# A GRU and a mixture of experts on one core: block 0's projections summed in the gates' banks, two seeds picked by matmul, and the rows of the last eight tiles fetched early

## The chip, the core and the metric

The kernel runs on one core of a Trainium2 chip. The metric is the device time of one execution in microseconds (us), as the median of the runs. A core has five engines that run their own instruction queues in order: TensorE (PE in the profile, PEld for its weight loads), VectorE (DVE), ScalarE (ACT), GpSimd (POOL) and SyncE (SP). SP does no arithmetic here: it issues DMA transfers. ACT and POOL can issue them too. An instruction waits in its queue until the semaphores it needs are set, and everything behind it in that queue waits with it.

## The reference

A gated recurrent cell (GRU) runs over T = 256 time steps for B = 8 sequences of width D = 512; its outputs go through a mixture of 8 experts, two chosen for each token, and through a shared expert; the input is added back.

```python
def cell(h, x):
    gi = x @ W_ih + b_ih
    gh = h @ W_hh + b_hh
    i_r, i_z, i_n = jnp.split(gi, 3, axis=-1)
    h_r, h_z, h_n = jnp.split(gh, 3, axis=-1)
    r = jax.nn.sigmoid(i_r + h_r)
    z = jax.nn.sigmoid(i_z + h_z)
    n = jnp.tanh(i_n + r * h_n)
    return (1.0 - z) * n + z * h

# per token of the GRU's outputs:
topk_w, topk_ids = jax.lax.top_k(softmax(x @ w_gate), 2)      # weights scaled to sum to 1
routed = sum over the two experts of weight * (silu(x @ up_gate) * (x @ up)) @ down
shared = (silu(x @ sh_gate) * (x @ sh_up)) @ sh_down
out = input + routed + shared
```

## The kernel before

All arithmetic is in 32-bit floats. The order of every engine's instructions is the order of the program's text (a manual schedule).

**The GRU.** Time is cut into 16 blocks of `TS` = 16 steps. `project(k, g)` makes the input projection of block k for gate g (0, 1, 2 for r, z, n): four pieces, one for each quarter q of the input width, each of four matmuls of 512 columns into one PSUM bank. The end of the last piece adds the bias and puts the result into an SBUF tile (`gi_first` for block 0, `gi_later` for all others), from which it is sent to memory, turned to another layout. From there `load_seeds(c)` brings it back in chunks of `SC` = 4 steps into `seeds` (r and z) and `seeds_n` (n); each has two buffers. `open_gate(n, g)` has ACT copy one step's seed into the gate's part of a PSUM bank (`banks`: "rn", "z" and "x"), and `step(n)` adds the recurrent matmuls on top of it (L518), then works out the new state on ACT and DVE. `step(n)` calls `open_gate(n + 1, ...)` for the step after it. POOL makes one small copy in each step (`last_hn`, L547).

Other work is laid between the steps: each step is given a share of a queue of pieces (projections of coming blocks, the shared expert), and `afterward` puts small pieces of VectorE work behind a step where there is room.

**The head** is all that comes before step 0. SP loads x's block 0 (`load_x_plain(0)`), three quarters of the input weights, the biases, the last quarter, x's block 1, the recurrent weights, and block 2. TensorE runs all twelve pieces of block 0 in three banks of the pool `ps_mm`, and DVE adds the bias to each gate (L434). ACT sends chunk 0 to memory (`send_first`, L461 and L463); `load_seeds(0)` brings it back, the z part by ACT and the n part by POOL. Meanwhile TensorE turns block 1 (`turn_x_plain(1)`) and runs ten pieces of block 1's projections. Then the three gates are opened, ACT issues six more sends (chunks 1 to 3), and step 0 begins.

**The expert tiles.** During the recurrence the tokens are ranked and their rows dealt, by indirect DMAs, into a table in memory (`dealt`) that is sorted by expert. After the recurrence, up to 39 tiles of 128 rows are run; the first 35 (`always`) always run. `fetch_rows(i)` loads a register on SP with the place of tile i's rows and issues four DMAs of 64 KB, into one of the three buffers of the pool `xpool`. `tile_unit(i)` has five parts: `before_` (DVE turns the rows, L912, and SP fetches tile i + 2), four up-matmuls (L782; L791 for tile 34) into a bank, the gating on ACT and DVE (L769, L773, L774), a turn (L808, L810), and two down-matmuls (L947; L940 for tile 34), after which DVE scales the result into a tile `y` with two buffers (L950; L941 for tile 34) and POOL adds it into `out` by an indirect DMA (L956). `run_tile` interleaves three tiles: tile i's `before_`, tile i - 1's up-matmuls, tile i - 2's turn and down-matmuls.

The list `routing` holds what is done between the last pieces of the shared expert, `fetch_rows(0)` and `fetch_rows(1)` last. When four pieces are left, `before_` of tiles 0 and 1 is done. The shared expert's last two results go to `out` by SP's stores in `add_up` (L884), at the end of these pieces.

Of the kernel before, what the change touches and what calls it, by code (L numbers as in the profile page):

```python
# [9 lines left out]
F32 = mybir.dt.float32  # L10
# [3 lines left out]
ALU = mybir.AluOpType  # L14
# [4 lines left out]
TS = 16  # L19
SC = 4  # L20
NS = 2
NH = 4


@with_exitstack
def kernel(
# [108 lines left out]
    load_x_plain(0)  # L135
    for q in range(NQ):
        if q == NQ - 1:
            nc.sync.dma_start(bias, b_ih.partition_broadcast(P))
            nc.sync.dma_start(bias_h, b_hh[0 : 2 * D].partition_broadcast(P))
        nc.sync.dma_start(wih[:, q], w_ih.rearrange("(p q) n -> q p n", q=NQ)[q])  # L140
    load_x_plain(1)
    w_hh_v = w_hh.rearrange("(q p) n -> p q n", p=P)
    for g in (0, 2, 1):
        cols = slice(g * D, (g + 1) * D)
# [150 lines left out]
    for j in range(4):  # L295
# [4 lines left out]
    for tile_ in seeds_n:  # L300
        nc.gpsimd.tensor_copy(tile_, seed_hn.unsqueeze(1).broadcast_to([P, SC, P]))


    rows = dram.tile([B, T, D], F32, name="rows")
# [8 lines left out]
    nc.gpsimd.memset(nothing, 0.0)  # L313
    load((listed[0:P], vacant), (listed[P : E * NM + 1], vacant[0 : E * NM + 1 - P]))
    load((dealt[E * NM], nothing))


    spare = deque()
# [75 lines left out]
    def bank_of(shape, name):  # L394
        if len(held) == 3:
            for needed in held[0]:
                needed()
        readers = []
        held.append(readers)
        return ps_mm.tile(shape, F32, tag="mm", name=name), readers  # L400

    def catch_up(room):
        while afterwards and (room is None or afterwards[0][0] <= room):
            cost, work = afterwards.popleft()
            work()
            if room is not None:
                room -= cost

    def project(k, g):

        box = {}

        def issue(q, cols):
            if q == 0 and cols.start == 0:
                if k in turned_x:
                    turned_x.pop(k)()
                box["ps"], _ = bank_of([P, D], f"gip_{k}_{g}")
            multiply(
                box["ps"][:, cols],
                lambda c: xT_of[k][:, c, q, :],  # L420
                wih[:, q, g * D + cols.start : g * D + cols.stop],
                start=(q == 0 and cols.start == 0),
                stop=(q == NQ - 1 and cols.stop == D),
            )

        def by_group(t_):
            return t_.rearrange("p (q j i) -> p j q i", q=NQ, j=4)

        def end():
            gi = gi_later if k else gi_first  # L430
            to_gi = gi[:, :, g, :].rearrange("p j (q i) -> p j q i", q=NQ)
            bias_g = by_group(bias[:, g * D : (g + 1) * D])
            if k == 0:
                nc.vector.tensor_tensor(to_gi, by_group(box["ps"]), bias_g, ALU.add)  # L434
            else:
                nc.scalar.copy(to_gi, by_group(box["ps"]))
                nc.gpsimd.tensor_tensor(to_gi, to_gi, bias_g, ALU.add)
            if g > 0:
                projected.add((k, "rzn"[g]))
            if g > 0 and k == 0:  # L440
                send_first(g, 0)
            elif g > 0:
                to = gi_dram[k][g % 2].rearrange("j b t n -> (b t) j n")
                if g == 1:
                    nc.sync.dma_start(to.rearrange("p j (a n) -> p j a n", a=2), gi[:, :, 0:2, :])
                else:
                    nc.sync.dma_start(to, gi[:, :, 2, :])
# [6 lines left out]
    projected = set()  # L454

    def send_first(g, c):

        rows_ = slice(SC * B * c, SC * B * (c + 1))
        to = gi_first_dram[g % 2][c].rearrange("j t b n -> (t b) j n")
        if g == 1:  # L460
            nc.scalar.dma_start(to.rearrange("p j (a n) -> p j a n", a=2), gi_first[rows_, :, 0:2, :])  # L461
        else:
            nc.scalar.dma_start(to, gi_first[rows_, :, 2, :])  # L463

    def load_seeds(c, of="nz"):

        k, o = divmod(c * SC, TS)
        steps = slice(o, o + SC)
        for g in of:
            assert (k, g) in projected  # L470
            tile_, at_row = (seeds_n[c % NS], B) if g == "n" else (seeds[c % NS], 0)
            for j in range(4):
                if k:
                    src = gi_dram[k][int(g != "n")][j, :, steps, :]
                else:
                    src = gi_first_dram[int(g != "n")][o // SC, j].rearrange("t b n -> b t n")
                by = nc.sync if c else nc.scalar if g == "z" else nc.gpsimd
                row = 32 * j + at_row
                by.dma_start(tile_[row : row + B], src)

    def open_gate(n, g):

# [406 lines left out]
        )  # L889

    xr_of = {}

    def fetch_rows(i):
        if i < NT:
            xr_of[i] = xpool.tile([P, NG, P], F32, tag="x", name=f"xr_{i}")
            at = nc.values_load(
                laid["steer"][0:1, NT + 1 + i : NT + 2 + i],
                engines=(mybir.EngineType.SP,),
                min_val=0,
                max_val=E * NM,  # L900
            )
            src = dealt[bass.ds(at, 1)].rearrange("o (g t) (j m) -> j t (o g) m", g=NG, j=4)
            for j in range(4):
                nc.sync.dma_start(xr_of[i][32 * j : 32 * j + 32], src[j])

    def tile_unit(i):
        box = {}
# [98 lines left out]


    nc.vector.transpose(states[0].rearrange("p q b -> p (q b)"), h.rearrange("p q i -> p (q i)"))
    nc.vector.tensor_tensor(bias[:, 0 : 2 * D], bias[:, 0 : 2 * D], bias_h, ALU.add)

    first = [project(0, g) for g in range(3)]
    for q in range(NQ):
        for g in range(3):
            first[g][q].run(None)
    catch_up(None)
    load_seeds(0, "z")
    load_seeds(0, "n")
    load_shared()

    projections = deque()  # L1020
    for k in range(1, NB):
# [11 lines left out]
    ahead_of_it = 2 * NQ + 2  # L1033
    while ahead_of_it:
        piece = projections.popleft()
        ahead_of_it -= piece.parts > 0
        piece.run(None)
    for g in gate_of:
        open_gate(0, g)
    for c in range(1, TS // SC):  # L1040
        for g in (1, 2):
            send_first(g, c)
    load_seeds(1)
    due = spent = 0.0
    to_enter = deque()
    for k in range(NB):
# [4 lines left out]
        def when(t, cost, busy, work):  # L1051
            at.setdefault(t, []).append((cost, busy, work))
# [13 lines left out]
            for i in range(2):  # L1066
                when(12 + late + 2 * i, 0, 0, lambda k=k, i=i: deal_rows(k - 1, i))
        for e in range(E):
            when(2 + e, 0, 0, lambda k=k, e=e: nc.sync.dma_start(
                dealt[e * NM + k].rearrange("p (a n) -> p a n", n=P),  # L1070
                blank.unsqueeze(1).broadcast_to([P, D // P, P]),
            ))
# [130 lines left out]
```

## Time and profile before

| | us |
|---|---|
| Median of three runs | 1394.12 (1392.59 to 1395.21) |
| The profiled execution's own time | 1392.42 |
| Its span, first to last instruction | 1390.3 |
| TensorE busy | 1369.6 |
| VectorE, ScalarE, GpSimd busy | 654.6, 473.8, 290.1 |

| Stretch of the span (us) | What runs there |
|---|---|
| 0 to 31.84 | the head |
| 31.84 to about 1145 | the 256 steps |
| to 1190.3 | the rest of the shared expert, routing of the last block |
| 1190.3 to 1380.1 | the 35 expert tiles on TensorE |
| 1383.24 | the last scatter into `out` is issued |

A row of the timeline has the start, the duration, the engine, the line, the operation, what it writes and reads, how often (merged rows), and in brackets how long the engine stood idle before it and what ended that. An engine's name with a q (SPq, ACTq) marks what its queue issues rather than what its arithmetic does. A row of the waits has the engine and line that waited, what it waited for, the total in us, how often, and the longest. A row of the windows has the stretch, its length, the busy time of PE, PEld, DVE, ACT and POOL, the granted TensorE clock, the share of the DMA engines, and GB/s.

### The profile page before, as it was taken

How to read it: one execution, taken by the hardware profiler on the slowest of the kernel's cores; microseconds unless marked ns; L12 is line 12 of the kernel's file. 1: busy time of each engine (PE TensorE's matmuls, PEld its weight loads, DVE VectorE, ACT ScalarE, POOL GpSimd, SP SyncE). 2: the span in 40 equal slices, each digit the busy share in tenths (PEclk: the TensorE clock that was granted, in tenths of full speed). 3: DMA queues.
4: the chain of work that ended last, by engine and by line, in shares of the span. 5: the costliest groups of instructions: out<-in, count | busy, mean ns of one | idle time of the engine just before them, and what ended most of it. 6: DMA issues, size and time to landing. Idle time of an engine off the chain costs nothing. (4 is left out here: it accounts for less than half of the span.)

```text
span 1390.3 us, 59000 instructions
## 1 busy us (share of the span) xinstructions
PE 1369.6 (99%) x24524; PEld 784.1 (56%) x24524; DVE 654.6 (47%) x2702; ACT 473.8 (34%) x2037; POOL 290.1 (21%) x564
## 2 busy tenths in 40 slices
PE   8999999999999999999999999999999999999996
PEld 3455556665656565656665566566656665444443
DVE  2445444545454544455544554554445543344442
ACT  0444443434343434343434343434343330111110
POOL 3333332121111111111111111111111132133332
PEclk9999999999999999999999999999999999999999
DMA  7545563333332232223222223232223445455553
GB/s 272 161 139 144 124 134 98 112 104 91 101 101 67 74 83 75 67 83 83 81 77 59 83 77 88 58 84 83 66 67 83 131 101 168 93 94 102 96 99 52
DMA packets 157490, 137.36 MB, mean 99 GB/s; under 512 B 17240, under 2 KB 133384, under 8 KB 157224
## 3 DMA queue, kind: packets, MB, share of 16 engines
q1 hardware_dynamic: 140680, 95.54, 24.6%
q0 software_dynamic: 15072, 37.11, 12.1%
q8 instruction: 194, 3.18, 1.0%
q10 hardware_dynamic: 1472, 0.93, 0.3%
q14 instruction: 72, 0.59, 0.1%
HBM read 61.00 MB, written 72.52 MB: 96 GB/s over the span
## 5 line engine op out<-in xcount | busy, mean ns | idle before, releaser
L518 PE MATMUL ps_rn<-we,hT 128*8 128x256 f32 x8192 | 490.5, 379 | 5.6 <-DVE hT L549 3.0
L518 PEld LDWEIGHTS ps_rn<-we,hT 128*8 128x8 f32 x8192 | 223.2, 89 | 254.6 <-ACT ps_z L490 51.2
L531 DVE STREAM_TRANSPOSE rT<-ps_rn 128x128 f32<-128x128 f32 x256 | 81.2, 317 | 434.5 <-PE ps_rn L518 434.5
L518 PE MATMUL ps_z<-we,hT 128*8 128x128 f32 x8192 | 272.2, 273 | 0.0
L518 PEld LDWEIGHTS ps_z<-we,hT 128*8 128x8 f32 x8192 | 227.5, 90 | 50.7
L535 ACT ACTIVATE rT<-rT 128x32 f32<-128x32 f32 x256 | 58.5, 229 | 527.7 <-DVE rT L531 519.7
L547 POOL COPY last_hn<-hn 128x1 f32<-128x1 f32 x256 | 46.8, 183 | 826.2 <-DVE hn L546 826.2
L845 PE MATMUL gu_s<-hc,wsu 128*32 128x256 f32 x3072 | 188.4, 379 | 0.0
L342 PE MATMUL gip<-we,xT 128*32 128x512 f32 (+2 forms) x1872 | 186.1, 522 | 1.6 <-DVE xT L220 1.6
L845 PEld LDWEIGHTS gu_s<-hc,wsu 128*32 128x32 f32 x3072 | 101.2, 110 | 58.5 <-issue 11.8
L342 PE MATMUL po<-wsd,act_s 128*32 128x512 f32 (+2 forms) x1272 | 130.2, 509 | 0.0
L782 PE MATMUL gu_t<-we,xrT 128*128 x272 | 127.8, 593 | 0.0
L342 PEld LDWEIGHTS gip<-we,xT 128*32 128x32 f32 x1872 | 59.9, 111 | 71.3 <-issue 61.5
L531 DVE STREAM_TRANSPOSE zT<-ps_z 128x128 f32<-128x128 f32 x256 | 79.0, 309 | 0.0
L552 ACT COPY hc<-hT 128x32 f32<-128x32 f32 x192 | 47.4, 247 | 90.9 <-DVE hT L549 90.9
L782 PEld LDWEIGHTS gu_t<-we,xrT 128*128 128x128 f32 x272 | 49.0, 190 | 49.6 <-issue 42.0
L490 ACT COPY ps_rn<-seeds_n 128x128 f32<-128x128 f32 x256 | 69.0, 269 | 9.2 <-DMA seeds_n<-gid_n_first 1.0
L538 DVE TENSOR_TENSOR rT<-nT,rT 128x32 f32<-128x32 f32 x256 | 50.3, 197 | 42.6 <-ACT rT L535 42.2
L531 DVE STREAM_TRANSPOSE nT<-ps_rn 128x128 f32<-128x128 f32 x256 | 70.2, 274 | 0.0
L490 ACT COPY ps_rn<-seeds 128x128 f32<-128x128 f32 x256 | 68.9, 269 | 2.3 <-DMA x<-in_x_dram 1.2
L950 DVE TENSOR_SCALAR y<-yp,share 128x512 f32<-128x512 f32 x34 | 25.5, 751 | 89.3 <-PE yp L947 60.1
L546 DVE TENSOR_TENSOR hn<-hT,rT 128x32 f32<-128x32 f32 x256 | 49.3, 193 | 38.5 <-ACT rT L541 11.1
(169 smaller groups left out, 1197.4 us busy)
## 6 DMA issues: line engine op xcount, KB each, us to landing
dealt<-blank SPq DMA_DIRECT2D x128, 256.0 KB
xr<-dealt SPq DMA_DIRECT2D x140, 64.0 KB
we<-in_L_ffn_w_gate_up_dram POOLq DMA_DIRECT2D x32, 256.0 KB, 4.3
gid_rz<-gi SPq DMA_DIRECT2D x15, 512.0 KB
seeds<-gid_rz SPq DMA_DIRECT2D x240, 32.0 KB
wsu<-_L_ffn_w_sh_gate_up_dram POOLq DMA_DIRECT2D x16, 256.0 KB, 4.1
rows<-hr SPq DMA_DIRECT2D x128, 32.0 KB
rb<-rows SPq DMA_DIRECT2D x16, 256.0 KB
```

Of the source, the lines that this page charges most:

```text
L342: nc.tensor.matmul(ps[32 * c : 32 * c + 32], lhs(c), rhs, start=start, stop=stop, skip_group_check=True,)
L490: nc.scalar.copy(gate_of[g], src)
L518: nc.tensor.matmul(banks[g][32 * j : 32 * j + B, 0 : n_ * P].rearrange("b (a k i) -> b a k i", a=n_, k=NQ), hT[:, q, 0:B], whh_v[:, q, j, ...
L531: nc.vector.transpose(gT.rearrange("p a b -> p (a b)"), gate_of[g])
L535: nc.scalar.activation(r, r, AF.Sigmoid)
L538: nc.vector.tensor_tensor(r, nT[:, :, 0:B], r, ALU.mult)
L546: nc.vector.tensor_tensor(hn, hT[:, :, 0:B], nn, ALU.subtract)
L547: nc.gpsimd.tensor_copy(last_hn, hn[:, 0, 0:1])
L552: nc.scalar.copy(hc_of_block(k).rearrange("p g q (c t) -> p q g c t", t=TS)[:, :, :, :, t], new.rearrange("p q (g c) -> p q g c", c=2),)
L782: nc.tensor.matmul(box["ps"], lhs(q), w_up(q), start=(q == 0), stop=(q == NQ - 1))
L845: nc.tensor.matmul(box["ps"][32 * g : 32 * g + 32, two_i, :], wsu[c][:, q, two_i, fs], hc_of[m][:, :, q, :], start=(two_i == 0 and q == 0) ...
L950: nc.vector.tensor_scalar(y, box["y"], laid["share"][:, i : i + 1], None, ALU.mult)
```

## The change

In the head, block 0's projections are summed in the gates' own banks instead of three of `ps_mm`, so that block 1's pieces can run between block 0's before block 0's banks have been read. x's block 1 is loaded ahead of the biases. All eight sends of block 0 go from ACT's queue to POOL's, right after the bias sums, and `load_seeds(0)`, also on POOL, loads only steps 2 and 3 of chunk 0. Steps 0 and 1 (`NP` = 2) no longer go through memory: `pick_seeds` multiplies `gi_first` by a matrix of ones and zeros (`pick`, made by POOL from the identity) that moves the rows of a step to the partitions where the seeds stand; ACT copies the r and z result to `seeds`, DVE adds the n result and the bias row into `seeds_n`. Block 1's bias sums go from POOL to DVE, as work behind a step. The stores of blank rows begin three steps later in block 0.

In the tiles, `rooms` cuts the seeds' buffers and `gi_later`, unused after the recurrence, into nine pieces of the size of a tile's rows. `fetch_far` fetches the next of the last eight tiles (27 to 34) into such a piece. Four calls stand in `routing` behind `fetch_rows(1)`, and one in every `before_`, behind its own fetch, while any are left. `fetch_rows` leaves out a tile that it has already.

```diff
@@ loads of the head
     for q in range(NQ):
         if q == NQ - 1:
+            load_x_plain(1)
             nc.sync.dma_start(bias, b_ih.partition_broadcast(P))
...
-    load_x_plain(1)
@@ the matrix that picks
+    pick = we[0 : SC * B, 2, 3, 0 : 6 * SC * B].rearrange("p (s m) -> p s m", s=SC)
+    nc.gpsimd.memset(pick, 0.0)
+    nc.gpsimd.tensor_copy(
+        pick[:, :, 2 * B : 3 * B], ident[0 : SC * B, 0 : SC * B].rearrange("p (s b) -> p s b", s=SC)
+    )
@@ project
-                box["ps"], _ = bank_of([P, D], f"gip_{k}_{g}")
+                if k == 0:
+                    box["ps"] = banks[("rn", "z", "x")[g]]
+                else:
+                    box["ps"], _ = bank_of([P, D], f"gip_{k}_{g}")
...
+            nc.scalar.copy(to_gi, by_group(box["ps"]))
+            if k == 1:
+                biased[g] = afterward(0.66, lambda: add_bias(nc.vector, to_gi, bias_g))
             else:
-                nc.scalar.copy(to_gi, by_group(box["ps"]))
-                nc.gpsimd.tensor_tensor(to_gi, to_gi, bias_g, ALU.add)
+                add_bias(nc.gpsimd, to_gi, bias_g)
@@ send_first and load_seeds
-            nc.scalar.dma_start(to, gi_first[rows_, :, 2, :])
+            nc.gpsimd.dma_start(to, gi_first[rows_, :, 2, :])
...
-                by.dma_start(tile_[row : row + B], src)
+                if c:
+                    nc.sync.dma_start(tile_[row : row + B], src)
+                else:
+                    nc.gpsimd.dma_start(tile_[row : row + B, NP:], src[:, NP:])
@@ new
+    def pick_seeds(s, gates, at, ps):
+        for j in range(4):
+            nc.tensor.matmul(
+                ps[32 * j : 32 * j + 32],
+                pick[:, s, at : at + 32],
+                gi_first[0 : SC * B, j, gates, :],
+                start=(s == 0),
+                stop=(s == NP - 1),
+                skip_group_check=True,
+            )
+
+    def first_seeds():
+        rz = banks["rn"].rearrange("p (s g n) -> p s g n", s=NP, g=2)
+        n = banks["x"][:, 0 : NP * P].rearrange("p (s n) -> p s n", s=NP)
+        for s in range(NP):
+            pick_seeds(s, slice(0, 2), 2 * B, rz[:, s])
+        for s in range(NP):
+            pick_seeds(s, slice(2, 3), B, n[:, s : s + 1])
+        nc.scalar.copy(seeds[0][:, 0:NP], rz.rearrange("p s g n -> p s (g n)"))
+        nc.vector.tensor_tensor(
+            seeds_n[0][:, 0:NP], n, seed_hn.unsqueeze(1).broadcast_to([P, NP, P]), ALU.add
+        )
@@ fetch_rows and fetch_far
+    rooms = [t_.rearrange("p s n -> p (s n)") for t_ in (*seeds, *seeds_n)]
+    rooms.append(gi_later.rearrange("p j g n -> p (j g n)"))
...
-    def fetch_rows(i):
-        if i < NT:
-            xr_of[i] = xpool.tile([P, NG, P], F32, tag="x", name=f"xr_{i}")
+    def fetch_rows(i, room=None):
+        if i < NT and i not in xr_of:
+            if room is None:
+                room = xpool.tile([P, NG, P], F32, tag="x", name=f"xr_{i}")
+            xr_of[i] = room
...
+    def fetch_far():
+        if far:
+            fetch_rows(far.popleft(), rooms.popleft())
...
             if i + 2 not in (always, always + 1):
                 fetch_rows(i + 2)
+            fetch_far()
@@ the head's order
+    first, second = [[project(k, g) for g in range(3)] for k in range(2)]
+    for q in range(NQ - 1):
+        for g in range(3):
+            first[g][q].run(None)
     turn_x_plain(1)
...
+    for q in range(NQ - 1):
+        second[0][q].run(None)
+    nc.vector.tensor_tensor(bias[:, 0 : 2 * D], bias[:, 0 : 2 * D], bias_h, ALU.add)
+    for g in range(3):
+        first[g][NQ - 1].run(None)
+    for c in range(TS // SC):
+        for g in (1, 2):
+            send_first(g, c)
+    load_seeds(0)
+    load_shared()
+    for q in range(NQ - 1):
+        second[1][q].run(None)
+    first_seeds()
     for g in gate_of:
         open_gate(0, g)
...
+    second[0][NQ - 1].run(None)
+    for q in range(NQ - 1):
+        second[2][q].run(None)
+    projections.extendleft(second[g][NQ - 1] for g in (2, 1))
+    catch_up(None)
+    turn_x_afterwards(2)
     load_seeds(1)
@@ the tiles' order
+    far.extend(range(always - 8, always))
...
         (22 * MM, lambda k: fetch_rows(0)), (22 * MM, lambda k: fetch_rows(1)),
+        *((22 * MM, lambda k: fetch_far()) for _ in range(4)),
```

More of the change, by code (lines that the diff above doesn't have):

```diff
@@ L21 @@
 NS = 2
+NP = 2
 NH = 4
@@ L299 @@
         )
-    for tile_ in seeds_n:
-        nc.gpsimd.tensor_copy(tile_, seed_hn.unsqueeze(1).broadcast_to([P, SC, P]))
     rows = dram.tile([B, T, D], F32, name="rows")
@@ L315 @@
     load((dealt[E * NM], nothing))
+    pick = we[0 : SC * B, 2, 3, 0 : 6 * SC * B].rearrange("p (s m) -> p s m", s=SC)
[3 more added lines that the diff above has]
+    )
+    for tile_ in seeds_n:
+        nc.gpsimd.tensor_copy(tile_, seed_hn.unsqueeze(1).broadcast_to([P, SC, P]))
     spare = deque()
@@ L434, in end, with add_bias @@
                 nc.vector.tensor_tensor(to_gi, by_group(box["ps"]), bias_g, ALU.add)
-            else:
-                nc.scalar.copy(to_gi, by_group(box["ps"]))
-                nc.gpsimd.tensor_tensor(to_gi, to_gi, bias_g, ALU.add)
[L438 to L447, printed above, removed]
+                if g > 0:
+                    projected.add((k, "rzn"[g]))
+                return
+            if g in biased:
+                biased.pop(g)()
+            nc.scalar.copy(to_gi, by_group(box["ps"]))
+            if k == 1:
+                biased[g] = afterward(0.66, lambda: add_bias(nc.vector, to_gi, bias_g))
+            else:
+                add_bias(nc.gpsimd, to_gi, bias_g)
+        def add_bias(engine, to_gi, bias_g):
+            engine.tensor_tensor(to_gi, to_gi, bias_g, ALU.add)
+            if g == 0:
+                return
+            projected.add((k, "rzn"[g]))
+            to = gi_dram[k][g % 2].rearrange("j b t n -> (b t) j n")
+            if g == 1:
+                nc.sync.dma_start(to.rearrange("p j (a n) -> p j a n", a=2), gi_later[:, :, 0:2, :])
+            else:
+                nc.sync.dma_start(to, gi_later[:, :, 2, :])
         return [
@@ L454 @@
     projected = set()
+    biased = {}
     def send_first(g, c):
@@ L460, in send_first, with load_seeds @@
         if g == 1:
-            nc.scalar.dma_start(to.rearrange("p j (a n) -> p j a n", a=2), gi_first[rows_, :, 0:2, :])
+            nc.gpsimd.dma_start(to.rearrange("p j (a n) -> p j a n", a=2), gi_first[rows_, :, 0:2, :])
         else:
-            nc.scalar.dma_start(to, gi_first[rows_, :, 2, :])
-    def load_seeds(c, of="nz"):
+            nc.gpsimd.dma_start(to, gi_first[rows_, :, 2, :])
+    def load_seeds(c):
         k, o = divmod(c * SC, TS)
-        steps = slice(o, o + SC)
-        for g in of:
+        steps = slice(o, o + SC) if c else slice(NP, SC)
+        for g in "nz":
             assert (k, g) in projected
@@ L476, in load_seeds @@
                     src = gi_first_dram[int(g != "n")][o // SC, j].rearrange("t b n -> b t n")
-                by = nc.sync if c else nc.scalar if g == "z" else nc.gpsimd
                 row = 32 * j + at_row
-                by.dma_start(tile_[row : row + B], src)
+                if c:
+                    nc.sync.dma_start(tile_[row : row + B], src)
+                else:
+                    nc.gpsimd.dma_start(tile_[row : row + B, NP:], src[:, NP:])
[20 more added lines that the diff above has]
+        )
     def open_gate(n, g):
@@ L891 @@
     xr_of = {}
-    def fetch_rows(i):
-        if i < NT:
-            xr_of[i] = xpool.tile([P, NG, P], F32, tag="x", name=f"xr_{i}")
+    rooms = [t_.rearrange("p s n -> p (s n)") for t_ in (*seeds, *seeds_n)]
+    rooms.append(gi_later.rearrange("p j g n -> p (j g n)"))
+    rooms = deque(
+        room[:, at : at + D].rearrange("p (g m) -> p g m", g=NG)
+        for room in rooms
+        for at in range(0, room.shape[1], D)
+    )
+    def fetch_rows(i, room=None):
[3 more added lines that the diff above has]
+            xr_of[i] = room
             at = nc.values_load(
@@ L904, in fetch_rows @@
                 nc.sync.dma_start(xr_of[i][32 * j : 32 * j + 32], src[j])
+    far = deque()
+    def fetch_far():
+        if far:
+            fetch_rows(far.popleft(), rooms.popleft())
     def tile_unit(i):
@@ L1008 @@
     nc.vector.transpose(states[0].rearrange("p q b -> p (q b)"), h.rearrange("p q i -> p (q i)"))
[L1009 to L1018, printed above, removed]
     projections = deque()
-    for k in range(1, NB):
+    for k in range(2, NB):
         for g in range(3):
@@ L1030, in turn_x_afterwards @@
         turned_x[k] = afterward(1.1, lambda: transpose_x(k))
-    turn_x_plain(1)
[L1033 to L1037, printed above, removed]
+        afterwards.rotate(1)
+    first, second = [[project(k, g) for g in range(3)] for k in range(2)]
+    for q in range(NQ - 1):
+        for g in range(3):
+            first[g][q].run(None)
+    turn_x_plain(1)
+    for q in range(NQ - 1):
[11 more added lines that the diff above has]
+    first_seeds()
     for g in gate_of:
         open_gate(0, g)
-    for c in range(1, TS // SC):
-        for g in (1, 2):
-            send_first(g, c)
+    second[0][NQ - 1].run(None)
[4 more added lines that the diff above has]
+    turn_x_afterwards(2)
     load_seeds(1)
@@ L1068 @@
         for e in range(E):
-            when(2 + e, 0, 0, lambda k=k, e=e: nc.sync.dma_start(
+            when(2 + e + 3 * (k == 0), 0, 0, lambda k=k, e=e: nc.sync.dma_start(
                 dealt[e * NM + k].rearrange("p (a n) -> p a n", n=P),
```

## The prediction

> **What bounds the kernel now.** I read the page's busy rows first, then TensorE's waits over the whole span, then the timeline of the two ends that the change touches.
>
> ```profile
> PE 1369.6 (99%) x24524; PEld 784.1 (56%) x24524; DVE 654.6 (47%) x2702; ACT 473.8 (34%) x2037; POOL 290.1 (21%) x564
> PE ps_rn L518 <- DVE hT L549: 3.0, 5, 1.3
> PE ps_rn L518 <- ACT ps_rn L490: 1.8, 1, 1.8
> ```
>
> TensorE is busy for all but 20.7 us, so the time can fall only by what lies before step 0, in a few holes, and after its last matmul; any new hole is paid in full. The two waits are the largest between head and end. The timeline of the head says where they come from:
>
> ```profile
> 30.20 0.27 ACT L490 COPY ps_rn<-seeds 128x128 f32<-128x128 f32 x1 [1.22 <-DMA x<-in_x_dram]
> 31.51 0.27 ACT L490 COPY ps_rn<-seeds_n 128x128 f32<-128x128 f32 x1 [1.04 <-DMA seeds_n<-gid_n_first]
> 31.84 1.91 PE L518 MATMUL ps_rn<-we,hT 128*8 128x256 f32 x32 [1.79 <-ACT ps_rn L490]
> 33.60 1.66 ACTq L461 DMA_DIRECT2D gid_rz_first<-we  x1
> 35.79 0.23 ACT L535 ACTIVATE rT<-rT 128x32 f32<-128x32 f32 x1 [3.81 <-DMA gid_rz_first<-we]
> 37.62 1.91 PE L518 MATMUL ps_rn<-we,hT 128*8 128x256 f32 x32 [1.28 <-DVE hT L549]
> 41.94 1.92 PE L518 MATMUL ps_rn<-we,hT 128*8 128x256 f32 x32
> ```
>
> Step 0 starts 1.79 us after the projections end, because the n seeds return late from memory. It then lasts 5.78 us (31.84 to 37.62) where step 1 lasts 4.32: ACT is issuing six sends until 35.75, and the sigmoid of step 0 stands behind them.
>
> The other end is the stretch of expert tiles. SP's timeline, one window per fetch:
>
> ```profile
> 1176.12 1.89 SPq L904 DMA_DIRECT2D xr<-dealt  x4
> 1178.82 2.24 SPq L904 DMA_DIRECT2D xr<-dealt  x4
> 1181.85 2.23 SPq L904 DMA_DIRECT2D xr<-dealt  x4
> 1187.23 2.98 SPq L904 DMA_DIRECT2D xr<-dealt  x4
> 1190.32 1.46 SPq L884 DMA_DIRECT2D out_dram<-again  x2
> 1195.27 1.86 SPq L904 DMA_DIRECT2D xr<-dealt  x4
> 1197.98 1.84 SPq L904 DMA_DIRECT2D xr<-dealt  x4
> ```
>
> A fetch occupies SP's queue from one start to the next: 2.70 us (1176.12 to 1178.82), 3.03 and 2.71 (1195.27 to 1197.98). Last, POOL and VectorE in that stretch, and the traffic of the two stores:
>
> ```profile
> 1194.00:1195.00 1.00, 1.00 (x4) 0.41 (x3) 0.51 (x2) 0.38 (x1) 0.00 (x0) 1.00 0.52 199
> 1195.00:1196.00 1.00, 1.00 (x5) 0.55 (x4) 0.96 (x2) 0.03 (x1) 0.00 (x0) 1.00 0.08 31
> 1200.27 1.62 POOL L956 DMA_INDIRECT out_dram<-y,row  x1 [0.72 <-DMA xr<-dealt]
> 1209.35 0.75 DVE L950 TENSOR_SCALAR y<-yp,share 128x512 f32<-128x512 f32 x1 [2.65 <-issue]
> 1210.57 0.42 DVE L773 TENSOR_TENSOR act_t<-gu_t,act_t 128x256 f32<-128x256 f32 x1 [0.46 <-ACT act_t L769]
> 1378.06 1.57 POOL L956 DMA_INDIRECT out_dram<-y,row  x1 [1.19 <-DMA out_dram<-y,row]
> 1383.24 1.57 POOL L956 DMA_INDIRECT out_dram<-y,row  x1 [2.30 <-POOLq L1169]
> DMA to landing us min/median/max: 4.8/5.0/6.1
> ```
>
> The stores of 1190.32 stop moving at about 1195.5, 5.2 us after their issue. Every scatter waits for the one before it to land; the last starts 2.3 us after its data are ready. The scatters are a second chain beside TensorE, with 5.38 us from one to the next ((1383.24 - 1200.27) / 34).
>
> **The head, part by part.** Removed: the 1.79 us hole, and 5.78 - 4.32 = 1.46 us in step 0, since the eight sends leave ACT. Both runs make 12 pieces of block 0 and 10 of block 1 before step 0, in another order, so the pieces cost nothing new. A piece is 0.88 us (80 matmul records, 8.79 us, are ten).
>
> Added on TensorE: eight pick matmuls of 256 columns and eight of 128. The nearest rows are a step's own: sixteen of 256 columns take 1.73 us (31.84 to the next group at 33.57), sixteen of 128 take 0.87. Half of each is 0.87 + 0.43 = **1.30 us**. Above, 32 unhidden weight loads at 111 ns (mean of L342's loads) would make it 3.5; the end below is nothing. I take 1.30, since the steps' loads do hide.
>
> The old first twelve pieces end at 19.7. Now nine end at 17.1, block 1's turn costs its 1.5 us as before, three pieces of block 1 follow, then the last three of block 0 (to 23.8), three more of block 1 (to 26.4), and the picks (to 27.7). The last bias sum (0.69) is done at 24.7, ahead of the picks. Behind them: an ACT copy of 128x512 (0.58, L436), a VectorE sum of 128x256 (0.42, L773), three gate copies (0.27 each): about 1.9 us, ready at 29.6. Four pieces (3.5 us) of block 1 hide it, to 31.15, when step 0 starts; without them it would cost 1.9. The input weights' last quarter, now behind x's second block (256 KB at some 400 GB/s, 0.65 us), is needed only at 21.2.
>
> POOL now issues eight sends and eight seed loads: sends at 0.62 to 0.73 (its load rows), 5.3 us from 23.9; loads at 0.55, 4.4 us; it is free at 33.6 and the last seeds land 2.3 us later, at 36. Step 1 opens the gates of step 2 at 35.5 + 2.6 = 38.1, so 2 us of slack; the POOL copy of step 0's hn, behind them, is due at 34.6. Cost taken: 0. Had each send the 1.66 us of the longest ACT issue, the seeds would be 5.5 us late; that is the upper end, and none are early. Here the Trainium skill speaks against the move: "DMA: Bandwidth & Descriptors", sections "Issuing engine by pattern" and "Specifications", calls the sync and scalar path generally faster than POOL's, and its first-byte figures (0.6 and 1 us) make the sends land some 0.4 us later, an estimate that stays inside the slack. Block 1's bias sums go from POOL (1.28) to VectorE (0.69 each, three), which waits 20.7 us for TensorE in the first 60 us: 0. The block of blank stores put three steps later costs SP nothing that anyone waits for. Head: -1.79 - 1.46 + 1.30 = **-2.0 us** (0.2 with the loads unhidden, -3.3 with free picks).
>
> **The tiles.** Eight fetches leave the last tiles, and are put where they stand ahead of other work on SP: four after those of tiles 0 and 1, one each behind the fetches of tiles 2 and 3, all six before the two stores of L884; two more with tiles 4 and 5. Each counts with its register load and four DMAs. Fetch ten (six far ones and 0 to 3) starts at 1181.85 + 7 x 2.87 (mean of 2.70, 3.03, 2.71 and a fourth of 3.0: the queue came to L904's semaphore wait at 1184.8 after the fetch of 1181.85) = 1201.9, the stores issue at 1204.0 instead of 1190.32, and land at 1209.3.
>
> What is queued behind: the first scatter writes the tensor that the stores write, so it waits for them and starts at 1209.6, not 1200.27. Tile 2's y takes the buffer of tile 0's (two of them), so VectorE's L950 waits until 1209.6 + 5.05 = 1214.7, where it ran at 1209.35. Behind L950 on VectorE stand the two gating products of tile 3 (0.88), which TensorE's transpose needs: 1214.7 + 0.75 + 0.88 + 0.2 = 1216.6 against 1211.7. **TensorE loses 4.9 us.** Tile 4's rows, fetched at about 1207.5 and landed at 1212, would alone cost some 2 us; they lie inside this wait. From there the scatters go on at about 5.37 us, as the tiles do, so the loss stays and doesn't grow.
>
> At the end nothing is fetched beside the last scatters. The last five gaps of before, already so, are 5.07 to 5.26 us, 0.25 under the tiles' 5.37; eight more such tiles take up to 2.0 us off the scatters' lag, which was 1.2 for the last but one. If it starts as before, 0.7 is gained; having started from the buffers' limit (about 4.7), it ends near where it was. I take 5.0 for the tiles. Bounds: 3.6 (2.70 a fetch, and 0.7 gained at the end), and 7.3 (the first scatter's 9.3 late, less 2.0, if the chain never gains elsewhere).
>
> A rule of the skill adds to it: "TensorE: Matmul & The Clock Gate", Part 1, says that an idle window of about 3.4 us halves the clock until a busy one passes. The clock row stays at 1.00 through the holes of the head, the longest 1.79 us, so this trace can't decide; by the rule the sum would be up to 1.7 us more.
>
> **Sum.** -2.0 + 5.0 = +3.0: a span of 1393.3. The profiled execution was 1392.42 with its 1390.3 span, 1.7 below the median of 1394.12; the same shift on the median gives **1397.1 us**.
>
> **Rivals.** *The far fetches cost no one anything* (ends faster). TensorE is untouched if the first scatter starts by 1204.2 (1209.35 - 5.05), that is if the six fetches delay the stores by under 8.3 us. SP had 2.3 idle before 1187.23, so each may take 1.8; the bare issues are 4 x 0.32 = 1.3. Against it: the measured 2.7 to 3.0. Time: 1394.1 - 2.0 - 0.7 = 1391.4. *The seeds of steps 2 and 3 come late* from POOL and eat the head's gain: for it, sixteen issues in one queue; against, 2 us of slack. 1394.1 + 5.0 = 1399.1. *The end isn't freed*: the scatters keep a lag of 3.5 because they started 9.3 late: 1394.1 - 2.0 + 7.3 = 1399.4; against it, the gaps of 5.1 at the end.
>
> **How the numbers follow.** Forecast 0.58, cheap fetches 0.20, late seeds 0.12, end not freed 0.10. About 0.2% (2.8 us) is what a measurement of this kernel can tell: the bounds are 1391.3 and 1396.9. The forecast lies on the upper one, so its chance splits about evenly between slower and the same, with 0.03 below; the first rival splits between faster and same; the others are slower. Faster 0.13, same 0.37, slower 0.50. The forecast's own range is 1394.5 to 1399.4. With the first rival below and 7.3 without the head's gain (1401.4) above, the range is 1391.4 to 1400.9.
>
> **What would show it.** Right: step 0 starts near 31.2 with no hole before it and step 1 4.3 us later; L884's stores issue near 1202 (all shifted by the head's 2), the first scatter 9 us later than its data, L950 of tile 2 waiting on a scatter, TensorE idle some 5 us in two holes there. Wrong: stores before 1198, or a gate copy waiting on seeds in step 1.

## The result, and the profile after

The changed kernel takes 1405.76 us (median of six runs, 1401.55 to 1410.05) against 1393.34 us (six runs, 1392.59 to 1395.21) for the kernel before on the same chip: a ratio of 1.0086, 95% interval [1.0076, 1.0095]. It is slower by about 12 us, where 3 were forecast. The profiled execution was the longest of the six: 1410.05 us, with a span of 1408.3.

Line numbers shift with the change: the step L518 is now L562, the gate copies L490 are L534, the turned rows L912 are L971, the up-matmuls L782 are L826, the turn L808 and its copy L810 are L852 and L854, the down-matmuls L947 are L1007, y L950 is L1010, the scatter L956 is L1016, the stores L884 are L928, and the fetch L904 is L957.

The busy rows of the page and the three longest waits of TensorE over the whole span of the changed kernel:

```profile
PE 1373.8 (98%) x24556; PEld 790.4 (56%) x24556; DVE 658.1 (47%) x2706; ACT 474.1 (34%) x2038; POOL 294.5 (21%) x575
```

```profile
PE yp L1007 <- ACT actT_t L854: 14.3, 1, 14.3
PE ps_rn L562 <- DVE hT L593: 4.1, 4, 1.7
PE ps_rn L208 <- DVE seeds L200: 2.3, 1, 2.3
```

One new wait of 14.3 us stands first. TensorE is also busy 4.2 us longer (1373.8 against 1369.6), of which the pick matmuls make some 1.4: some of its work ran slower. The head of the changed kernel, TensorE's and ACT's rows from its timeline:

```profile
29.01 1.91 PE L562 MATMUL ps_rn<-we,hT 128*8 128x256 f32 x32
33.33 1.91 PE L562 MATMUL ps_rn<-we,hT 128*8 128x256 f32 x32
...
37.64 0.27 ACT L534 COPY ps_rn<-seeds 128x128 f32<-128x128 f32 x1 [1.70 <-DMA seeds<-gid_rz_first]
39.56 1.91 PE L562 MATMUL ps_rn<-we,hT 128*8 128x256 f32 x32 [1.73 <-DVE hT L593]
```

Both holes of before are gone: no wait stands ahead of step 0, and it lasts 4.32 us (29.01 to 33.33) instead of 5.78. Step 1, though, lasts 6.23 us, because the seeds of step 2 were 1.70 us late.

At the tiles, SP's timeline of the changed kernel (the rooms bear the names of the tensors they were cut from, seeds and seeds_n):

```profile
1180.63 4.54 SPq L957 DMA_DIRECT2D xr<-dealt  x8
1186.05 10.90 SPq L957 DMA_DIRECT2D seeds<-dealt  x16
1197.74 1.84 SPq L957 DMA_DIRECT2D xr<-dealt  x4
1200.36 1.84 SPq L957 DMA_DIRECT2D seeds_n<-dealt  x4
1203.04 1.84 SPq L957 DMA_DIRECT2D xr<-dealt  x4
1205.67 1.84 SPq L957 DMA_DIRECT2D seeds_n<-dealt  x4
1207.62 1.43 SPq L928 DMA_DIRECT2D out_dram<-again  x2
```

Ten fetches of four DMAs stand ahead of the two stores, 2.62 to 2.73 us each from one start to the next, with one of 3.69, and the stores go out at 1207.62 instead of 1190.32. Who waits for them is in the rows of ACT, TensorE and POOL:

```profile
1195.20 0.38 ACT L813 ACTIVATE act_t<-gu_t 128x256 f32<-128x256 f32 x1 [8.37 <-PE gu_t L826]
1211.82 0.37 ACT L854 COPY actT_t<-ps_x 128x256 f32<-128x256 f32 x1 [16.23 <-DMA out_dram<-again]
1212.24 3.78 PE L1007 MATMUL yp<-we,actT_t 128*128 x4 [14.28 <-ACT actT_t L854]
1215.82 3.99 PE L826 MATMUL gu_t<-we,xrT 128*128 x6
1217.79 1.62 POOL L1016 DMA_INDIRECT out_dram<-y,row  x1 [0.72 <-DMA gi<-dealt]
```

The waiter is neither the scatter nor tile 2's y. It is ACT's copy L854 of tile 0, the first tile. Its target `actT` is allocated in the pool `two` under the tag "again", and so are the shared expert's results that the two stores read: both stand in the same two buffers. The copy can't write until the store has landed. In the trace of before, the tiles' start and the same copy were:

```profile
1190.30 5.42 PE L782 MATMUL gu_t<-we,xrT 128*128 x12
1195.97 0.37 ACT L810 COPY actT_t<-ps_x 128x256 f32<-128x256 f32 x1 [1.55 <-DVE xrT L912]
```

There the stores went out with the tiles' start, and the copy waited for no store. In the changed kernel, when the scatter comes, at 1217.79, the stores have long landed; it starts 0.72 us behind the work before it on POOL, as before (0.72).

The windows of the same stretch (PE, PEld, DVE, ACT and POOL busy, then the granted clock) show the second loss:

```profile
1190.00:1200.00 10.00, 7.96 (x32) 3.01 (x24) 2.23 (x4) 0.38 (x1) 0.00 (x0) 1.00 0.33 96
1200.00:1212.00 12.00, 0.00 (x0) 0.00 (x0) 0.71 (x1) 0.18 (x1) 0.00 (x0) 0.55 0.38 109
1212.00:1220.00 8.00, 7.76 (x13) 3.40 (x14) 2.21 (x4) 0.57 (x2) 1.80 (x2) 0.60 0.31 89
1220.00:1230.00 10.00, 10.00 (x27) 4.39 (x25) 3.65 (x7) 1.51 (x4) 2.36 (x4) 1.00 0.73 148
```

Behind the hole the granted clock is 0.60 for 8 us. The four down-matmuls take 3.78 us instead of 1.88, the next six up-matmuls 3.99 instead of 2.74: 3.15 us on top of the hole.

The two profiled spans differ by 18.0 us (1408.3 - 1390.3), and this is where they lie:

| Stretch | us |
|---|---|
| up to the start of step 2 (39.56 against 41.94) | -2.4 |
| steps 28 to 31 (20.94 against 17.83) | +3.1 |
| the hole behind the stores | +14.3 |
| slow clock behind it | +3.15 |
| last scatter behind its data (1.28 against 2.30) | -1.0 |
| all other steps and stretches, together | +0.9 |

Steps 28 to 31 were in no part of the prediction; they are taken up with the last experiments.

### The profile page after: what moved, and what is told of

Read it like the earlier page. It is cut to its first block, busy times and chain, and to the rows that moved or that the text cites. A ratio compares the mean times of both kernels' runs of the same rounds, so it can differ in the third digit from the quotient of the medians.

```text
span 1408.3 us, 59054 instructions
## 1 busy us (share of the span) xinstructions
PE 1373.8 (98%) x24556; PEld 790.4 (56%) x24556; DVE 658.1 (47%) x2706; ACT 474.1 (34%) x2038; POOL 294.5 (21%) x575
## 5 line engine op out<-in xcount | busy, mean ns | idle before, releaser
L562 PE MATMUL ps_rn<-we,hT 128*8 128x256 f32 x8192 | 491.8, 379 | 4.9 <-DVE hT L593 4.1
L562 PEld LDWEIGHTS ps_rn<-we,hT 128*8 128x8 f32 x8192 | 225.7, 89 | 252.3 <-ACT ps_z L534 52.1
L562 PE MATMUL ps_z<-we,hT 128*8 128x128 f32 x8192 | 274.0, 273 | 0.1
L562 PEld LDWEIGHTS ps_z<-we,hT 128*8 128x8 f32 x8192 | 228.7, 90 | 50.5 <-issue 0.4
L348 PE MATMUL gip<-we,xT 128*32 128x512 f32 (+3 forms) x1776 | 175.3, 512 | 1.7 <-issue 0.9
L826 PE MATMUL gu_t<-we,xrT 128*128 x272 | 129.1, 598 | 0.0
L1007 PE MATMUL yp<-we,actT_t 128*128 x136 | 65.8, 607 | 14.3 <-ACT actT_t L854 14.3
L826 PEld LDWEIGHTS gu_t<-we,xrT 128*128 128x128 f32 x272 | 49.6, 192 | 51.0 <-issue 42.7
L1010 DVE TENSOR_SCALAR y<-yp,share 128x512 f32<-128x512 f32 x34 | 25.5, 751 | 101.2 <-issue 79.7
L534 ACT COPY ps_rn<-seeds_n 128x128 f32<-128x128 f32 x256 | 69.0, 269 | 8.3 <-DVE seeds_n L521 0.2
L534 ACT COPY ps_rn<-seeds 128x128 f32<-128x128 f32 x256 | 68.9, 269 | 3.3 <-DMA seeds<-gid_rz_first 1.7
```

The source lines that it names most:

```text
L348: nc.tensor.matmul(ps[32 * c : 32 * c + 32], lhs(c), rhs, start=start, stop=stop, skip_group_check=True,)
L534: nc.scalar.copy(gate_of[g], src)
L562: nc.tensor.matmul(banks[g][32 * j : 32 * j + B, 0 : n_ * P].rearrange("b (a k i) -> b a k i", a=n_, k=NQ), hT[:, q, 0:B], whh_v[:, q, j, ...
L826: nc.tensor.matmul(box["ps"], lhs(q), w_up(q), start=(q == 0), stop=(q == NQ - 1))
L1007: nc.tensor.matmul(box["y"], lhs, rhs, start=(f == 0), stop=(f == NF - 1))
L1010: nc.vector.tensor_scalar(y, box["y"], laid["share"][:, i : i + 1], None, ALU.mult)
```

## The experiments

In the expectations, H is the theory read from the trace above (late stores hold the shared buffers), R its rival there. Ratios are against the kernel before, run on the same chip.

| Kernel | us, median | ratio, 95% interval |
|---|---|---|
| head alone | 1389.18 | 0.9981 [0.9971, 0.9991] |
| far fetches alone | 1406.55 | 1.0105 [1.0088, 1.0123] |
| last stores on ACT's queue | 1397.45 | 1.0028 [1.0013, 1.0044] |
| far fetches behind the stores | 1389.44 | 0.9982 [0.9972, 0.9991] |
| buffers of their own for the turned results | 1397.35 | 1.0029 [1.0017, 1.0041] |
| two far fetches ahead of the stores | 1393.07 | 1.0001 [0.9990, 1.0013] |
| last stores on POOL's queue | 1392.51 | 0.9998 [0.9987, 1.0010] |
| head alone, first seeds loaded earlier | 1397.47 | 1.0031 [1.0020, 1.0041] |

### The two halves apart

The head alone is the changed kernel without the list of far tiles; all rows are fetched as before.

```diff
-    far.extend(range(always - 8, always))
```

> The change without its far fetches (the list of far tiles stays empty). Theory H (the time was lost in the tiles alone): step 2 starts 2.4 us earlier than before and this is kept to the tiles, so 1393.3 - 2.4 = 1390.9 us. Rival R (the head's order also costs time later, as the profile of the change loses 3.7 us in steps 28 to 31): those steps again last 5.1 to 6.1 us instead of 4.32, and the time is about 1394.5.

The far fetches alone are the kernel before with `rooms`, `fetch_far`, its calls in `routing` and in `before_`, and nothing of the new head.

> The kernel before with the far fetches alone. Theory H: the same hole as in the changed kernel, 10 to 14 us of TensorE waiting at tile 0's down-matmul, and about 3 us of half clock behind it, less 1 us at the end: 1404 to 1409. Rival R: less than half of the 12.4 us is lost here, under 1399.

Measured: the head alone gains 0.19%, some 2.6 us; the far fetches alone lose 1.05%, some 14.6 us. The halves add up: 14.6 - 2.6 = 12.0, and the whole change lost 0.86%, which is 12.0 too. The far fetches alone have the same waits as the whole change, from the tile's view and the waits of that kernel (there the copy is L810, the down-matmul L964):

```profile
L884 SPq DMA_DIRECT2D out_dram<-again x2: 617/668/719, 1205.0 to 1205.8; - x2
```

```profile
PE yp L964 <- ACT actT_t L810: 12.3, 1, 12.3
```

The stores go out 14.7 us later than before (1205.0 against 1190.32) and TensorE waits 12.3 us. In the head alone and in all kernels with timely stores no wait of TensorE between 1185 and 1385 is longer than 0.5 us.

### The stores moved past the fetches

First, the last two stores go out on ACT's queue:

```diff
-            nc.sync.dma_start(out[:, k * TS : (k + 1) * TS, :], xt)
+            by = nc.scalar if k >= NB - 2 else nc.sync
+            by.dma_start(out[:, k * TS : (k + 1) * TS, :], xt)
```

> The changed kernel, but the shared expert's last two stores are issued by ACT, whose queue is empty there. Theory H (the stores stand behind six far fetches on SP, and tile 0's turned result waits for their buffers): the hole at tile 0 goes away; tile 4's rows still come some 2 us late; 1391 to 1396. Rival T (the fetches' traffic or tile 2's late rows make the hole): the hole stays, over 1401.

Most of the loss is gone (1.0028 instead of 1.0086), but the time is above what H expected. ACT's and TensorE's rows of this kernel say why:

```profile
1196.27 1.67 ACTq L929 DMA_DIRECT2D out_dram<-again  x2
1200.87 0.38 ACT L813 ACTIVATE act_t<-gu_t 128x256 f32<-128x256 f32 x1 [14.28 <-DMA out_dram<-again]
1202.95 0.37 ACT L854 COPY actT_t<-ps_x 128x256 f32<-128x256 f32 x1 [1.70 <-PE ps_x L852]
```

```profile
PE ps_x L852 <- DVE act_t L818: 5.6, 1, 5.6
```

The two results were ready by 1192.1, yet ACT's queue stood at its first store until 1196.22. The trace shows there a wait on a semaphore that SP's far fetches had been using: in this program the DMAs of SP's and ACT's queues take turns in one set of semaphores, so a store on ACT's queue can still wait for a fetch on SP's. Behind the second store came a register load of 2.80 us, and only then tile 0's sigmoid (1200.87). The hole is now 5.6 us and at another place.

On POOL's queue, whose DMAs use other semaphores in the trace:

```diff
+            by = nc.gpsimd if k >= NB - 2 else nc.sync
```

> The full change, but the last two stores go out on POOL's queue, past SP's far fetches. Theory S: the stores land before 1197, tile 0's copy waits under 2 us; tile 2's rows stay late (landed at 1201 in the full change), which costs 2 to 5 us at tile 2. Time 1391 to 1397. Rival M (as with the stores on ACT's queue, the semaphores that the queues share hold the store back until a far fetch has landed, and what stands behind it on POOL, the first scatter, with it): a hole of 5 us or more, 1397 to 1402.

The hole is gone. POOL's rows of this kernel:

```profile
1189.75 0.70 POOL L929 DMA_DIRECT2D out_dram<-again  x1 [16.12 <-DVE again L927]
1190.62 0.63 POOL L929 DMA_DIRECT2D out_dram<-again  x1 [0.17 <-issue]
...
1200.18 1.70 POOL L1017 DMA_INDIRECT out_dram<-y,row  x1 [0.73 <-issue]
```

The stores wait for their data alone, and the first scatter starts 0.73 us behind the work before it on POOL, as before (0.72). TensorE's longest wait behind 1190 is 0.5 us; the rows of tile 2, still behind the far fetches, cost 0.17 us, not the 2 to 5 of the expectation. By the ratios the kernel is still 0.17%, some 2.4 us, slower than the head alone. Its profile is 3.4 us longer than that of the head alone (spans of 1389.8 and 1386.4), and 2.0 of them stand long before any far fetch: 1.54 in step 1, where the seeds came late, and 0.44 in steps 28 to 31. Ten runs gave 1388.56 to 1396.5, a spread of 8 us where the head alone has 3; what makes it, the one profile doesn't show.

Then the stores stay on SP, and all far fetches go behind them:

```diff
-            fetch_far()
+            if i > 1:
+                fetch_far()
...
-        *((22 * MM, lambda k: fetch_far()) for _ in range(4)),
```

> The changed kernel with the same eight far fetches, but begun with tile 2, behind the stores in SP's queue, one for each tile up to tile 9. Theory H: no hole at tile 0, the scatters' lag is gone by the end: 1390 to 1393. Rival T (any far fetch beside the first tiles costs, wherever it stands): over 1397.

Measured 0.9982, the head alone 0.9981. In place behind the stores, the far fetches cost nothing and gain nothing that these runs can tell (the intervals are 0.1% to either side).

### The dose

Two far fetches, those of the first two `before_`, ahead of the stores:

```diff
-        *((22 * MM, lambda k: fetch_far()) for _ in range(4)),
```

> The full change with two far fetches ahead of the two stores instead of six (the four of the routing left out, so only two rooms fewer are read ahead). Theory S with 2.9 us of SP for each fetch: the stores are issued 5.7 us later than before instead of 17, land at about 1200 where tile 0's copy wants the buffer at about 1197: a hole of 2 to 4 us, with little or no slow clock behind it. Time 1391 to 1395. Rival T (any far fetch ahead of the tiles costs the whole 14 us): 1400 or more. Rival 0 (no cost up to two): 1389 to 1390.5.

The stores, and who waits, in this kernel's tile view and timeline:

```profile
L928 SPq DMA_DIRECT2D out_dram<-again x2: 623/672/722, 1194.7 to 1195.5; - x2
```

```profile
1198.90 0.37 ACT L854 COPY actT_t<-ps_x 128x256 f32<-128x256 f32 x1 [3.39 <-DMA out_dram<-again]
1199.32 1.98 PE L1007 MATMUL yp<-we,actT_t 128*128 x4 [1.44 <-ACT actT_t L854]
```

A hole of 1.44 us, some less than expected, and next to no slow clock behind it (1.98 instead of 1.88). By the ratios this kernel is 0.20%, some 2.8 us, slower than the head alone; the hole accounts for about half of that, and the rest is open. With the others, a second profile of the whole change (told below) among them, this makes a line of slope one, when the first store's issue is counted from the first up-matmul of tile 0:

| | store behind the tiles' start, us | hole, us | difference |
|---|---|---|---|
| two far fetches ahead | 3.30 (1194.69 - 1191.39) | 1.44 | 1.86 |
| whole change, second profile | 13.89 (1202.29 - 1188.40) | 12.01 | 1.88 |
| far fetches alone | 14.26 (1205.00 - 1190.74) | 12.33 | 1.93 |
| whole change | 16.16 (1207.62 - 1191.46) | 14.28 | 1.88 |

In all four, tile 0's copy starts 4.14 to 4.21 us after the store's issue, and every microsecond beyond some 1.9 is a microsecond of TensorE. Before, the store went out 0.02 us behind the tiles' start (1190.32 and 1190.30). So 1.9 us were to spare: less than one fetch.

### The shared buffers taken away

The turned results get two buffers of their own, cut from the ninth piece of `rooms`, which no far tile uses; nothing else changes, and the stores stay late:

```diff
-            actT = two.tile([P, NF, P], F32, tag="again", name=f"actT_{name}")
+            actT = own[0]
+            own.rotate(1)
...
+    last = rooms.pop()
+    own = deque((last[:, 0:NF, :], last[:, NF : 2 * NF, :]))
```

> The full change, but the tiles' turned results (actT) get two buffers of their own instead of sharing two with the last results that the two late stores read. Theory S (shared buffers): the 14 us hole at tile 0's ACT copy goes; the stores stay as late as in the full change (about 1207), so what is left are the next things that are late: tile 2's rows (landed at 1201.3 in the full change, needed at about 1199) and the first scatter behind the stores with tile 2's y behind it, the wait that the prediction named (about 5 us, with a slower clock behind it up to 7). Time 1393 to 1399, and the first wait over 2 us of TensorE behind 1190 is at tile 2, not at tile 0. Rival Q (the queue or the transfers themselves are slow, the buffers have no part): the hole stays at tile 0, 1402 to 1410.

This kernel's rows of SP, POOL, VectorE and TensorE, put together from its timelines:

```profile
1209.35 1.62 POOL L1019 DMA_INDIRECT out_dram<-y,row  x1 [10.74 <-DMA out_dram<-again]
...
1211.73 0.71 DVE L974 STREAM_TRANSPOSE xrT<-xr 128x512 f32<-128x512 f32 x1 [6.59 <-DMA xr<-dealt]
1214.56 0.75 DVE L1013 TENSOR_SCALAR y<-yp,share 128x512 f32<-128x512 f32 x1 [2.12 <-DMA out_dram<-y,row]
...
1212.59 2.77 PE L826 MATMUL gu_t<-we,xrT 128*128 x4 [3.42 <-DVE xrT L974]
1216.16 0.69 PE L852 MATMUL ps_x<-ident,act_t 128*128 128x128 f32 x2 [0.80 <-DVE y L1013]
1216.64 1.91 PE L826 MATMUL gu_t<-we,xrT 128*128 x2
1218.35 2.92 PE L1010 MATMUL yp<-we,gi 128*128 x4
```

The wait at tile 0 is gone, though the stores are as late as ever: they go out 13.69 us behind the tiles' start (1203.05 - 1189.36; 13.89 in the second profile of the whole change). The time falls by 0.57% of before (1.0029 instead of 1.0086). With the nearer wait out of the way, the chain of the prediction appears: the first scatter, held by the stores, at 1209.35 (predicted 1209.6); tile 4's rows at 1211.73 (1212); tile 2's y, held by that scatter, at 1214.56 (1214.7); the transposes at 1216.16 (1216.6). The agreement is to a microsecond rather than to the tenth, since the tiles start 0.94 us earlier here than in the trace of before, from which the forecast counted: against the tiles' start each is 0.5 to 0.8 us later than forecast. TensorE loses 3.42 us at tile 4's rows and 0.80 at the transposes, together 4.2 (predicted 4.9; the expectation of this run had put the first wait at tile 2). Some 3.1 us more go to a slow clock: 2.77, 0.69, 1.91 and 2.92 us for groups that take 1.9, 0.38, 1.02 and 1.88.

### The seeds of steps 2 and 3

The head alone, with POOL's loads of these seeds put right behind the first chunk's two sends, ahead of the other six:

```diff
         for g in (1, 2):
             send_first(g, c)
-    load_seeds(0)
+        if c == 0:
+            load_seeds(0)
```

> The head alone (no far fetches), with the two loads of the picked seeds issued on POOL right behind the first chunk's sends, ahead of the work on the later chunks. Theory L (the seeds of steps 2 and 3 land late: ACT waited 1.70 us for them in the full change's profile, 0.2 to 0.6 in the others): the wait is gone, 0.2 to 1.9 us faster than the head alone (1389.2): 1387.3 to 1389. Rival N (POOL's order gives nothing, since the loads wait for the sends' landing either way): 1388.7 to 1389.7; if the loads hold up POOL's work on the second chunk instead, 1390 to 1391.

Far off: by the ratios (1.0031 and 0.9981) some 7 us slower than the head alone. Three rows of this kernel, from POOL's, ACT's and TensorE's timelines:

```profile
29.24 2.24 POOL L499 DMA_DIRECT2D seeds_n<-gid_n_first  x4 [6.01 <-DMA gid_n_first<-we]
...
48.64 0.58 ACT L449 COPY gi<-gip 128x512 f32<-128x512 f32 x1 [6.15 <-DMA gid_rz<-gi]
...
52.08 3.60 PE L562 MATMUL ps_rn<-we,hT 128*8 128x256 f32 x32 [5.19 <-DVE hT L593]
```

The loads are issued at 29.24, no earlier than in the head alone (29.18): they wait for the first sends to land, and POOL stands 6 us in front of them. The six other sends, which had gone out in that time, now go at 33.69 to 36.96. Chunk 1's loads on SP wait for them, so SP's queue runs 7 to 8 us late; in it stands the store of block 1's projections (45.58 instead of 38.35), whose landing ACT's next copy into `gi_later` awaits; behind that one on ACT stand step 3's sigmoid (49.13) and the gate copies of step 4. TensorE loses 5.19 us and again a slow clock (3.60 instead of 1.91).

### Second profiles

The whole change, the far fetches behind the stores, and the head alone ran once more, on one chip, for a second profile each.

> The full change once more, for a second profile. The steps 28 to 31 took 20.94 us together in its first profile, 17.83 in that of before, and in the other kernels with the new head between 17.36 and 20.77. Theory P (bound to the program, the ones with far fetches in the routing being 18.99 to 20.94): 20 to 21 again. Theory X (it varies from execution to execution): anywhere from 17.4 to 21. The hole at tile 0's ACT copy: 12 to 15 us again, with the four down matmuls behind it at 3.5 to 3.9 instead of 1.88. Time 1401 to 1410.

> The change with the far fetches behind the stores once more (no edit against the first run of it). Steps 28 to 31 took 17.36 us in its first profile. Theory P: 17.3 to 17.6 again; theory X: anywhere from 17.4 to 21, and the time then 1389.4 plus up to 3. No hole at the tiles in either.

> The head alone once more. Steps 28 to 31 took 18.55 us in its first profile. Theory P: 18.4 to 18.7 again; theory X: anywhere from 17.4 to 21. The start: 9 pieces of the first projection ended at 14.7 in its first profile, at 16.87 in the one with the stores on ACT; if the first matmuls' clock varies between executions, one of the two here too, and step 0 at 29.0 or at 31.15.

They took 1403.08, 1387.95 and 1390.93 us, the kernel before 1391.24. Steps 28 to 31 took 18.66, 17.37 and 19.40 us, where the first profiles had 20.94, 17.36 and 18.55: they vary between executions of one program, so P falls, though the kernel with the fetches behind was short both times. Part of it is a stand of TensorE before the same matmul of a projection, 0.3 to 1.1 us in the profiles that have it, for which the profile names no releaser ("issue"). In the first profile of the whole change:

```profile
157.49 1.06 PE L348 MATMUL gip<-we,xT 128*32 128x512 f32 x8 [0.92 <-issue]
```

The profiles of the two kernels with the old head, 17.83 and 17.71, don't have it. What causes it, and the rest of the loss in these steps, stays open.

In the second profile of the whole change, the stores go out at 1202.3, the hole is 12.01 us, and the four down-matmuls take 3.54 us:

```profile
1206.91 3.54 PE L1007 MATMUL yp<-we,actT_t 128*128 x4 [12.01 <-ACT actT_t L854]
1210.29 2.74 PE L826 MATMUL gu_t<-we,xrT 128*128 x6
```

Against the fetches behind the stores this is nearly a full account: 12.01 of hole, 1.66 of slow clock (3.54 - 1.88) and 1.29 in steps 28 to 31 make 14.96 us; the spans differ by 15.1 (1401.3 - 1386.2).

## Why the prediction was wrong

The sign was right and the size was not: 1397.1 was forecast, up to 1400.9, and 1405.76 measured.

**The head** (-2.0 forecast) held. The head alone gained 2.6 us (interval 1.3 to 4.0). The steps of the sum show in the kernel with the stores on ACT, whose first matmuls ran like those of before: nine pieces end at 16.87 (17.1 forecast), step 0 starts at 31.15 and step 1 at 35.47 (31.15 and 35.5); step 2 starts 1.93 us earlier than before (40.01 against 41.94). That kernel's rows:

```profile
16.87 0.75 PE L219 MATMUL xTp<-ident,x 128*128 128x128 f32 x4
31.15 1.91 PE L562 MATMUL ps_rn<-we,hT 128*8 128x256 f32 x32
35.47 1.91 PE L562 MATMUL ps_rn<-we,hT 128*8 128x256 f32 x32
```

The changed kernel's own profile starts step 0 2.1 us earlier still, since its first matmuls took 1.06 us a group from 6.86 on, where in others the same groups took 1.94 until about 10 or 11.

**The seeds** ("2 us of slack, cost taken: 0") held for the start that was forecast and not for an earlier one. The sum counted POOL's issues and forgot that the loads wait for the sends to land. In the kernel with the stores on ACT, where step 0 starts at 31.15 as forecast, POOL stands 1.04 us before the loads (29.65), the last of these seeds lands at 36.96 (forecast 36), and the copy that needs it runs without a wait:

```profile
38.09 0.27 ACT L534 COPY ps_rn<-seeds 128x128 f32<-128x128 f32 x1
```

That is 1.1 us of slack. Where step 0 starts before 29.1, the copy is due two microseconds earlier, POOL stands up to 3.5 us before the loads (3.37 in the changed kernel), and ACT waits up to 1.70 us; the sign that the prediction named for being wrong, a gate copy waiting for seeds in step 1, did appear there. (Step 1 is 0.2 us longer in every kernel with the new head, also where ACT waits for no seeds; why is not known.) So the seeds take back part of what the early start gives, and the rival of late seeds, which cancelled the head's gain, was wrong.

**SP's queue** held: ten fetches before the stores, 27.0 and 28.1 us from the first fetch to the first store in the two profiles of the whole change (27.9 forecast). The stores were to issue "near 1202" and did so at 1202.3 and 1207.62. The second is later because its first fetch started at 1180.63 instead of 1174.15, behind a slow deal: POOL's last deal stood 7.66 us for the one before it to land, against 5.08 in the other profile and 2.90 before. This queue now sets the end of a hole, so whatever shifts it enters the time. The runs spread wider, 8.5 us against 2.6 before; that fits, but isn't shown to come from it, since the kernel with the stores on POOL's queue has no such hole and spreads by 8 us.

**The step that failed** is the one behind it: "What is queued behind: the first scatter writes the tensor that the stores write [...] Tile 2's y takes the buffer of tile 0's". The prediction asked who writes what the stores write. It didn't ask who writes what the stores *read*. Their two source buffers come round to tile 0's turned result under the tag "again", and that copy runs at 1195.97 in the trace of before, where the first store had landed by about 1194.5 (an estimate: some 4.2 us after its issue, as in the four runs above). So the first waiter comes 13 us before the one that was named (y at 1209.35), and in place of the term of 4.9 us stood a hole of 12.0 to 14.3. The run with separate buffers shows it: with this one link cut, 1397.35 us were measured and the forecast chain ran within a microsecond of its forecast times. The agreement with 1397.1 is partly luck, since 3.1 us of slow clock, which the forecast left out, are in it.

**The end** ("0.7 is gained", or nothing) came out as nothing: fetches behind the stores run as fast as no far fetches. The scatters' lag of 2.3 us seems to have been that execution's own: in the head alone, with all its fetches in the old place, the last scatter is 1.15 us behind, in the changed kernel 1.28.

**The clock.** The trace of before held no hole long enough to test the rule of the Trainium skill ("TensorE: Matmul & The Clock Gate", Part 1), and the sum left its 1.7 us out. The runs agree with it: after idle stretches of 3.4, 5.6, 12.0 and 14.3 us TensorE's next groups took up to twice their time, for 1.6 to 3.2 us of loss (a granted clock of 0.60 for 8 us behind the longest), and after 1.44 us only 0.1. The sum's own wait of 4.9 us was over the rule's length, so the term belonged in it.

The rival of free far fetches needed the stores to slip by under 8.3 us; the line of doses puts the point at 1.9.

## What to carry to other kernels

When a store moves back in its queue, list both sides of it: who waits to write or read its destination, and who takes over its source buffer. A pool's tag is the place to look, since two tiles with unlike names can share buffers there. Then find the earliest of these waiters, by the time at which each wants the buffer, and compare it with the landing: here 1.9 us were to spare, and one fetch of 2.7 us uses that up.

A fetch put "far ahead" on a queue that issues in order is ahead of everything that is issued behind it there; what it gains at its own end has to be waited for somewhere before it is worth that. Here nothing waited for these rows, and the version to keep is the new head with the fetches left where they were.

## What the hardware showed that was not expected

- A store put on ACT's queue still waited for SP's fetches, from 1192.1, when its data were there, to 1196.22, through a semaphore that the program gives to the two queues' DMAs in turn; on POOL's queue, with semaphores of its own, it did not.
- The clock at the start differs between executions of one program: the head alone started step 0 at 29.01 in one profile and at 30.87 in another. Its first groups of matmuls took 1.06 us in the one and 1.94 in the other, and the trace's record of the full clock begins at 6.4 and at 10.7.
- Eight small loads of 0.56 us, put ahead of six sends on POOL, cost some 7 us: through POOL, SP's chunk loads and its store, and ACT's copy, to TensorE.
